# A planned instruction order in which GpSimd and VectorE take turns

## The chip, the core and the metric

The kernel runs on one core of a Trainium2 chip. The metric is the device time of one execution, in microseconds. Before the change it was 10084.26 us, the median of three runs (10083.36 to 10087.48). The engines are called by their names or as the profile abbreviates them: PE is TensorE (matrix products and transposes), PEld its weight loads, DVE is VectorE, ACT is ScalarE, POOL is GpSimd, SP is SyncE, which issues the transfers.

## What is computed

The input is a batch of 8 images of 256 channels and 32 x 32 points, in float32. Four layers follow each other, each on the output of the one before:

- Layer 0: a normalisation over channels, attention with 4 heads over the 1024 points (with a 3 x 3 depthwise convolution of the values added as positional term) and a projection, added to the input; then a second normalisation, a 1 x 1 convolution to 1024 channels, a 3 x 3 depthwise convolution, a gelu gate, a 1 x 1 convolution back to 256 channels, and a filter in the Fourier domain of 8 x 8 patches, added again.
- Layer 1: group normalisation, attention with 8 heads, projection, and a small two-layer network with gelu, each with a residual.
- Layer 2: a bottleneck of 1 x 1, 3 x 3 and 1 x 1 convolutions on values rounded to 8 bits, with a residual.
- Layer 3: a selective state-space scan in four directions over the points of each image (rows and columns, forward and backward), with 512 inner channels and 16 states each. For each state the recurrence h[t] = h[t-1] * exp(dt[t] * A) + dt[t] * u[t] * B[t] runs over the points, and the output is the sum over states of h[t] * C[t]. The four directions are summed.

## The kernel before

The work is cut into two phases that follow each other. `phase_a` takes the 8 images ("samples") through layers 0, 1 and 2 and leaves the 8-bit codes of each in DRAM. `phase_b` does layer 3.

The order of the instructions is not the order of the source. Each piece of work is a Python generator (a strand) that yields operations; class `_Order` holds all strands and makes the lists of all engines while the program is built. Each operation is an `_Op` (line 103): an engine, what it reads and writes, and `cost`, its expected duration in microseconds. The price is a formula in n, the largest number of columns of an operand divided by 1024, chosen by engine and kind of operation (lines 112 to 136). `start` (line 237) gives the earliest planned time of an operation: the engine must be free, and what it reads and overwrites must be done, with a latency for what another engine did. `run` (line 306) always emits the operation with the smallest planned start, and among equals the one of the smaller rank, then advances the engine's free time by the price. `keep_dense` (line 269) adds filler matmuls (line 295, weights `minus`) where the plan leaves TensorE idle for long. On the chip each engine then works through its list in order, and waits on semaphores only for data and buffers; the planned times are not in the program.

In phase A up to three samples are under way at once. The eight PSUM banks (`bank`) are shared by the attention and by everything else. For the softmax, `maxima` (line 603) computes scores into banks, VectorE takes their maxima from there (`stats`), ScalarE the exponentials in place; `exponentials` (line 669) computes the scores again with the maximum subtracted, takes exponentials into `exps`, and sums values into a bank. Where such a sum is complete, `finish` (line 799) in layer 0 adds it to the positional term: on VectorE if that term is ready, otherwise by way of a ScalarE copy and a GpSimd addition into `big`. The 3 x 3 depthwise convolutions are sums of nine shifted and scaled images. `outer_taps` (line 738) does a tap on two engines, a ScalarE scaling into `mid` and a GpSimd addition; it serves the positional term (tile `big`) and two of the eight chunks of the feed-forward part (tile `mid`). The other six chunks (line 888) do a tap in one VectorE `scalar_tensor_tensor` on tiles `mid`, of 31 x 31 = 961 or 992 columns. The normalisations (`rms`, line 519) and the rounding of layer 2 are VectorE work on SBUF too.

In phase B there are 64 blocks (8 images, 4 directions, 2 halves of 512 points), each of 16 groups, one per state. For a group, ScalarE makes `dbu` and `da`, TensorE transposes `dbu` into PSUM (`db`), VectorE scans four times 512 points (`h`), GpSimd multiplies h by C in two instructions of 1024 columns (line 1585), and TensorE sums the products into `py`. Between these run the preparations of the next blocks, through the PSUM tile `pp`: projections, a causal convolution with a VectorE `scalar_tensor_tensor` that reads PSUM, dt and its softplus, and the copies to `du`.

Of the kernel before, what the change touches and what calls it, by code (L numbers as in the profile page):

```python
# [22 lines left out]
BF16 = mybir.dt.bfloat16  # L23
# [3 lines left out]
PSUM = bass.MemoryType.PSUM  # L27
# [46 lines left out]
@with_exitstack  # L74
def tile_conv_seq(ctx: ExitStack, tc: tile.TileContext, i: dict, out: bass.AP):
    nc = tc.nc
    const = ctx.enter_context(tc.tile_pool(name="const", bufs=1))


    cols = const.tile([P, NCOL], F32, name="cols", tag="cols")  # L80
    nc.sync.dma_start(cols, i["cols"])

    def col(name, k=0, n=1):
        a = _AT[name][0] + k
        return cols[:, a : a + n]

    ident = const.tile([P, P], F32, name="ident", tag="ident")
    make_identity(nc, ident)
    dram = ctx.enter_context(tc.tile_pool(name="cd", bufs=1, space=DRAM))
    codes = [  # L90
        [dram.tile([CC, P, N], BF16, name=f"codes{b}_{k}", tag=f"codes{b}_{k}") for k in range(2)] for b in range(B)
    ]

    parts = [dram.tile([P, CC, 3, P], BF16, name=f"w_in{m}", tag=f"w_in{m}") for m in range(2 * DC)]

    phase_a(tc, i, col, ident, codes, parts)
    phase_b(tc, i, col, ident, codes, parts, out)


class _Op:  # L100


    def __init__(self, engine, method, args, kw):
        self.engine, self.method, self.args, self.kw = engine, method, args, kw
        out, ins = args[0], [a for a in (*args[1:], *kw.values()) if isinstance(a, bass.AP)]
        self.reads = {k for a in ins for k in self.blocks(a)}
        self.writes = {k for a in (out, kw.get("accum_out")) if a is not None for k in self.blocks(a)}
        self.landing = 0.0
        n = max(math.prod(a.shape[1:]) for a in (out, *ins)) / 1024
        near = all(a.space == out.space and out.space != PSUM for a in ins)  # L110
        points = sum(math.prod(a.shape[1:]) == 1 for a in ins)
        if engine == "tensor":
            x = kw.get("rhs", ins[0])
            n = math.prod(x.shape[1:]) / 1024
            self.rows = x.shape[0] / P * n * (0.427 if x.dtype != F32 else 1.707)
            move = method == "transpose" or kw.get("is_transpose", False)
            self.cost = max(0.05, n * (0.427 if x.dtype != F32 else 0.854 if move else 1.707))
            self.rows *= 0.5 if move else 1
        elif engine == "vector":
            fast = near and method in ("tensor_scalar", "tensor_copy")  # L120
            both = near and method == "tensor_tensor"
            three = near and method == "scalar_tensor_tensor"
            if method == "tensor_tensor_scan":
                self.cost = 0.03 + 2.15 * n + 0.05 * points
            elif both or three:
                self.cost = 0.04 + 1.53 * n
            elif fast:
                self.cost = 0.04 + 0.87 * n
            else:
                self.cost = 0.05 + 1.12 * n + 0.06 * min(points, 1)  # L130
        elif engine == "scalar":
            self.cost = 0.04 + 0.054 * near + 0.852 * n + 0.093 * points + 0.1 * ("accum_out" in kw)
        elif engine == "gpsimd":
            self.cost = 0.12 + 2.3 * n if method == "tensor_tensor" else 0.07 + (2.0 if out.dtype == BF16 else 1.5) * n
        else:
            self.cost, self.landing = 0.06, 3.6

# [12 lines left out]
class _Table:  # L150


    engine, reads, writes, cost, landing = "scalar", set(), set(), 1.3, 0.0

    def emit(self, nc):
        nc.scalar.preload_act_table_set("natural_log_exp_and_others")  # L156
# [27 lines left out]
class _Order:  # L184
# [7 lines left out]
    def __init__(self, nc):  # L192
        self.nc, self.strands, self.n = nc, [], 0
        self.free, self.written, self.read, self.base, self.last = {}, {}, {}, {}, {}
        self.rooms, self.minus, self.way, self.rows, self.fresh = [], None, 0.0, [], {}
        self.window, self.dense, self.half = 0, 0.0, False

    def add(self, rank, strand):
        self.n += 1
# [36 lines left out]

    def start(self, ops):
        e = ops[0].engine
        t = self.free.get(e, 0.0)
        for o in ops:  # L240
            for k in o.reads | o.writes:
                t = max(t, self.base.get(k[0], 0.0))
                w, by = self.written.get(k[0], {}).get(k, (0.0, e))
                t = max(t, w + (self.LATENCY[by] if by != e else 0.0))
            for k in o.writes:
                w, by = self.read.get(k[0], {}).get(k, (0.0, e))
                t = max(t, w + (self.LATENCY[by] if by != e else 0.0))
        return t
# [57 lines left out]
    def run(self):  # L306
        while self.strands:
            moved = True
            while moved:
                moved = False  # L310
                for s in list(self.strands):
                    if callable(s[2]) and s[2]():
                        self.go(s)
                        moved = True
            ready = [s for s in self.strands if not callable(s[2])]
            if not ready:
                assert not self.strands, [s[0] for s in self.strands]
                return
            t, s = min(((self.start(s[2][1]), s) for s in ready), key=lambda x: (x[0], x[1][0]))
            cost, ops = s[2]  # L320
            e = ops[0].engine
            if self.rooms and e == "tensor":
                t, cost = self.keep_dense(t, cost, ops)
            for o in ops:
                o.emit(self.nc)
                for k in o.reads:
                    self.read.setdefault(k[0], {})[k] = (t + cost + 0.7 * o.landing, e)
                for k in o.writes:
                    self.fresh.pop(k[0], None)
                    self.written.setdefault(k[0], {})[k] = (t + cost + o.landing, e)  # L330
            self.free[e] = t + cost
            self.go(s)


@with_exitstack
def phase_a(ctx, tc, i, col, ident, codes, w_parts):
# [783 lines left out]
    class _Table:  # L1120


        engine, reads, writes, cost, landing = "scalar", set(), set(), 1.3, 0.0

        def emit(self, nc):
            nc.scalar.preload_act_table_set("natural_log_exp_and_others")
# [675 lines left out]
```

## Time and profile before

| what | before |
| --- | --- |
| median of three runs | 10084.26 us |
| the profiled execution's own time | 10081.69 us |
| its span, first to last instruction | 10079.9 us |
| mean granted TensorE clock | 0.974 |
| busy: PE, ACT, DVE, POOL | 92%, 84%, 78%, 61% |
| phase A, to about 3540 us: PE, ACT, DVE, POOL busy | 3290, 2614, 2287, 954 us |
| phase B, 6540 us: PE, ACT, DVE, POOL busy | 6033, 5898, 5538, 5227 us |

An engine's busy time is the time in which at least one of its instructions runs; matmuls overlap each other, and the fillers count as busy. A line of a group of instructions names the source line (147 for all that the planner emits), the engine, the operation, the tiles as out<-in, their shapes, and the count; then the busy time in us and the mean duration of one in ns; then the engine's idle time just before these instructions, and what ended it. A window's line gives its bounds, its length, the busy time of each engine with the number of instructions, the granted TensorE clock, the share of the transfer engines, and GB/s. The slices are fortieths of the span; a digit is the busy share in tenths.

### The profile page before, as it was taken

Reading aid. Unit: us, or ns where it says so; the run is one execution under the profiler, and the core shown is the slowest. Engines: PE = TensorE matmul, PEld = TensorE weight load, DVE = VectorE, ACT = ScalarE, POOL = GpSimd, SP = SyncE. Lnnn points to the kernel's source line nnn. Section 1 sums busy time; section 2 is a strip of 40 time slices with the busy share of each in tenths; the row PEclk is TensorE's granted clock in tenths of the full one; section 3 lists DMA queues with packets and bytes.
Section 4 is the critical chain, followed back from the end, with each engine's and each line's share of the span. In section 5 each row is a group of like instructions: output and inputs, shape, how many; then the busy total and the mean of one; then the engine's idle time right before and its main releaser. Section 6 shows DMA issues by size and latency. Waiting matters only on the chain.

```text
span 10079.9 us, 152800 instructions
## 1 busy us (share of the span) xinstructions
PE 9322.4 (92%) x56655; PEld 5929.6 (59%) x56777; DVE 7825.8 (78%) x8666; ACT 8512.0 (84%) x15878; POOL 6180.5 (61%) x2998
## 2 busy tenths in 40 slices
PE   9988989989999989999999999999999999999998
PEld 3333333333333357777777777777777777777776
DVE  6476586586666568888888888888888888888788
ACT  8987765868677679998999998999898999898998
POOL 1454023142211068887878787878787878787888
PEclk9999999999999999999999999999999999999999
DMA  2100000000000011111111111112111111111111
GB/s 60 36 27 25 7 22 14 18 27 17 13 18 18 9 49 50 52 50 55 53 45 61 46 53 54 49 50 60 44 56 49 55 50 50 55 52 47 58 44 54
DMA packets 219628, 416.01 MB, mean 41 GB/s; under 512 B 25137, under 2 KB 67505, under 8 KB 213762
## 3 DMA queue, kind: packets, MB, share of 16 engines
q1 hardware_dynamic: 218882, 406.24, 13.1%
q8 instruction: 447, 7.32, 0.3%
q14 instruction: 299, 2.45, 0.1%
HBM read 358.43 MB, written 37.22 MB: 39 GB/s over the span
## 4 chain that ended last, share of the span: by engine, by line
PE 28%; ACT 22%; DVE 11%; issue 3%; DMA 1%; POOL 1%; DVEq 0%; SPq 0%; POOLq 0%; ACTq 0%
PE pp L147 12%; DVE h L147 9%; ACT da L147 9%; PE py L147 8%; PE db L147 8%; ACT dbu L147 7%; ACT L147 2%; ACT xs L147 2%; ACT dt L147 1%; DMA wi<-w_in 1%; ACT L156 1%; DVE du L147 1%; POOL h L147 1%; ACT st L147 0%; DVE ys L147 0%
## 5 line engine op out<-in xcount | busy, mean ns | idle before, releaser
L147 POOL TENSOR_TENSOR h<-h,cb 128x1024 f32<-128x1024 f32 x2048 | 4813.4, 2374 | 971.5 <-DVE h L147 441.0
L147 ACT ACTIVATE da<-dt,am 128x512 f32<-128x512 f32 x4096 | 2873.3, 714 | 452.2 <-DVE h L147 444.3
L147 ACT ACTIVATE dbu<-du,bT 128x512 f32<-128x512 f32 x4096 | 2800.5, 709 | 53.2 <-PE db L147 48.3
L147 PE MATMUL db<-ident,dbu 128*128 128x128 f32 x16384 | 2400.5, 278 | 390.2 <-DVE h L147 336.1
L147 DVE TENSOR_TENSOR_SCAN h<-da,db 128x512 f32<-128x512 f32 x2048 | 2344.5, 1201 | 439.4 <-ACT da L147 181.6
L147 DVE TENSOR_TENSOR_SCAN h<-da,st,db 128x512 f32<-128x512 f32 x2048 | 2465.1, 1260 | 263.2 <-ACT da L147 153.6
L147 PEld LDWEIGHTS db<-ident,dbu 128*128 128x128 f32 x16384 | 1871.7, 142 | 950.7 <-DVE h L147 526.5
L147 PE MATMUL py<-ident,h 128*128 128x128 f32 x16384 | 2095.8, 274 | 34.1 <-POOL h L147 33.2
L147 PEld LDWEIGHTS py<-ident,h 128*128 128x128 f32 x16384 | 1849.6, 141 | 97.0 <-POOL h L147 55.4
L147 DVE TENSOR_REDUCE stats<-bank 128x1 f32<-128x512 f32 x1536 | 972.0, 681 | 400.7 <-PE bank L147 394.2
L147 ACT ACTIVATE bank<-bank,stats 128x512 f32<-128x512 f32 x1536 | 1025.4, 714 | 266.6 <-DVE stats L147 261.7
L147 POOL TENSOR_TENSOR mid<-mid,mid 128x961 f32<-128x961 f32 (+2 forms) x192 | 402.3, 2103 | 966.9 <-ACT mid L147 661.9
L147 ACT ACTIVATE exps<-bank 128x512 f32<-128x512 f32 x1536 | 801.9, 636 | 144.8 <-PE bank L147 143.8
L147 PE MATMUL bank<-big,big 32*128 32x512 f32 x4096 | 845.0, 650 | 14.4 <-ACT bank L147 8.4
L147 PE MATMUL pp<-xi,cvd 128*128 128x512 f32 x1488 | 687.9, 598 | 6.3 <-DVE dt L147 6.3
L147 DVE SCALAR_TENSOR_TENSOR mid<-mid,cols,mid 128x961 f32<-128x961 f32 (+1 forms) x384 | 629.2, 1639 | 5.9
L147 PE MATMUL bank<-exps,big 128*32 128x512 f32 (+1 forms) x3072 | 565.2, 627 | 0.7 <-ACT exps L147 0.6
L147 PEld LDWEIGHTS bank<-big,big 32*128 32x128 f32 x4096 | 295.6, 187 | 429.8 <-issue 213.2
L147 POOL TENSOR_SCALAR big<-big,ga,gs 128x512 f32<-128x512 f32 x64 | 74.5, 1176 | 750.6 <-DVE gs L147 292.5
L147 POOL TENSOR_TENSOR tmp<-dt,xs 128x512 f32<-128x512 f32 x256 | 322.8, 1272 | 320.5 <-ACT dt L147 209.6
L147 POOL TENSOR_TENSOR big<-big,mid 128x961 f32<-128x961 f32 (+1 forms) x128 | 326.2, 2556 | 302.1 <-ACT mid L147 279.9
L295 PEld LDWEIGHTS <-minus 128*128 128x128 bf16 x2233 | 210.0, 101 | 446.7 <-issue 263.2
(207 smaller groups left out, 9792.7 us busy)
## 6 DMA issues: line engine op xcount, KB each, us to landing
cb<-c_d SPq DMA_DIRECT2D x1024, 256.0 KB, 3.2
wi<-w_in SPq DMA_DIRECT2D x192, 192.0 KB, 3.5
big<-in_x_dram SPq DMA_DIRECT2D x16, 1024.0 KB, 5.3
kept<-big SPq DMA_DIRECT2D x16, 1024.0 KB, 4.3
big<-kept SPq DMA_DIRECT2D x16, 1024.0 KB, 4.8
xf<-codes SPq DMA_DIRECT2D x48, 256.0 KB, 4.1
big<-big SPq DMA_DIRECT2D x16, 512.0 KB, 6.4
codes<-low SPq DMA_DIRECT2D x32, 256.0 KB, 2.0
```

The costliest lines, as they stand in the source:

```text
L147: return getattr(getattr(nc, self.engine), self.method)(*self.args, **self.kw)
L156: nc.scalar.preload_act_table_set("natural_log_exp_and_others")
L295: self.nc.tensor.matmul(x, lhsT=self.minus, rhs=rhs, start=True, stop=True)
```

## The change

The planner gets other prices, and one more resource. Each operation has a new attribute `port`. It is true for all GpSimd operations, and for those VectorE operations whose operands of more than one column all lie in SBUF (for a scan, the output is not looked at; the statistics of the group normalisation are left out). `start` lets an operation with `port` begin no earlier than the end of the last one with `port`, of whichever of the two engines, and `run` keeps that end. Prices change for VectorE operations on SBUF alone (two tensor inputs; scalar operations and copies), and for GpSimd's two-tensor operations. The kernel's computations, tiles, buffers and transfers are not edited.

```diff
@@ -105,7 +105,7 @@
         out, ins = args[0], [a for a in (*args[1:], *kw.values()) if isinstance(a, bass.AP)]
         self.reads = {k for a in ins for k in self.blocks(a)}
         self.writes = {k for a in (out, kw.get("accum_out")) if a is not None for k in self.blocks(a)}
-        self.landing = 0.0
+        self.landing, self.port = 0.0, engine == "gpsimd"
         n = max(math.prod(a.shape[1:]) for a in (out, *ins)) / 1024
         near = all(a.space == out.space and out.space != PSUM for a in ins)
         points = sum(math.prod(a.shape[1:]) == 1 for a in ins)
@@ -117,21 +117,23 @@
             self.cost = max(0.05, n * (0.427 if x.dtype != F32 else 0.854 if move else 1.707))
             self.rows *= 0.5 if move else 1
         elif engine == "vector":
+            wide = [a for a in ins if math.prod(a.shape[1:]) > 1] + [out] * (method != "tensor_tensor_scan")
+            self.port = not method.startswith("bn_") and all(a.space != PSUM for a in wide)
             fast = near and method in ("tensor_scalar", "tensor_copy")
             both = near and method == "tensor_tensor"
             three = near and method == "scalar_tensor_tensor"
             if method == "tensor_tensor_scan":
                 self.cost = 0.03 + 2.15 * n + 0.05 * points
             elif both or three:
-                self.cost = 0.04 + 1.53 * n
+                self.cost = 0.06 + 1.11 * n
             elif fast:
-                self.cost = 0.04 + 0.87 * n
+                self.cost = 0.05 + 0.56 * n + 0.05 * min(points, 1)
             else:
                 self.cost = 0.05 + 1.12 * n + 0.06 * min(points, 1)
         elif engine == "scalar":
             self.cost = 0.04 + 0.054 * near + 0.852 * n + 0.093 * points + 0.1 * ("accum_out" in kw)
         elif engine == "gpsimd":
-            self.cost = 0.12 + 2.3 * n if method == "tensor_tensor" else 0.07 + (2.0 if out.dtype == BF16 else 1.5) * n
+            self.cost = 0.12 + 2.2 * n if method == "tensor_tensor" else 0.07 + (2.0 if out.dtype == BF16 else 1.5) * n
         else:
             self.cost, self.landing = 0.06, 3.6
 
@@ -150,7 +152,7 @@
 class _Table:
 
 
-    engine, reads, writes, cost, landing = "scalar", set(), set(), 1.3, 0.0
+    engine, reads, writes, cost, landing, port = "scalar", set(), set(), 1.3, 0.0, False
 
     def emit(self, nc):
         nc.scalar.preload_act_table_set("natural_log_exp_and_others")
@@ -193,7 +195,7 @@
         self.nc, self.strands, self.n = nc, [], 0
         self.free, self.written, self.read, self.base, self.last = {}, {}, {}, {}, {}
         self.rooms, self.minus, self.way, self.rows, self.fresh = [], None, 0.0, [], {}
-        self.window, self.dense, self.half = 0, 0.0, False
+        self.window, self.dense, self.half, self.port = 0, 0.0, False, 0.0
 
     def add(self, rank, strand):
         self.n += 1
@@ -236,7 +238,7 @@
 
     def start(self, ops):
         e = ops[0].engine
-        t = self.free.get(e, 0.0)
+        t = max(self.free.get(e, 0.0), self.port if ops[0].port else 0.0)
         for o in ops:
             for k in o.reads | o.writes:
                 t = max(t, self.base.get(k[0], 0.0))
@@ -329,6 +331,8 @@
                     self.fresh.pop(k[0], None)
                     self.written.setdefault(k[0], {})[k] = (t + cost + o.landing, e)
             self.free[e] = t + cost
+            if ops[0].port:
+                self.port = t + cost
             self.go(s)
 
 
@@ -1120,7 +1124,7 @@
     class _Table:
 
 
-        engine, reads, writes, cost, landing = "scalar", set(), set(), 1.3, 0.0
+        engine, reads, writes, cost, landing, port = "scalar", set(), set(), 1.3, 0.0, False
 
         def emit(self, nc):
             nc.scalar.preload_act_table_set("natural_log_exp_and_others")
```

What the built program's lists become, in counts: phase A has 1163 filler matmuls where there were 1299, phase B 992 where there were 934. Six of the 64 attention sums of layer 0 that VectorE added are copied by ScalarE and added by GpSimd instead. All other instructions are the same in number. Position by position and without the fillers, another instruction stands in 4487 of TensorE's 6754 places in phase A, and in 10235 of its 39296 in phase B; for VectorE in 2240 of 3290 and 789 of 5378, for ScalarE in 2560 of 4193 and 2666 of 10151, for GpSimd in 339 of 485 and 10 of 2518.

## The prediction

> **What bounds the kernel now.** I read the page's slices first: where they change character, phase A (samples through layers 0 to 2) gives way to phase B (the scans of layer 3).
>
> ```profile
> PE   9988989989999989999999999999999999999998
> DVE  6476586586666568888888888888888888888788
> ACT  8987765868677679998999998999898999898998
> POOL 1454023142211068887878787878787878787888
> ...
> PE 28%; ACT 22%; DVE 11%; issue 3%; DMA 1%; POOL 1%; DVEq 0%; SPq 0%; POOLq 0%; ACTq 0%
> ```
>
> POOL jumps in slice 15, at about 3540 us. The chain of waits (last line) starts there too, so it speaks for phase B alone: 66% of the span, PE, ACT and DVE taking turns, POOL 1%. Phase A is read from its windows: all instructions, then L295 alone (filler matmuls that the list puts where it expects TensorE idle). Columns: window, length, PE, PEld, DVE, ACT, POOL busy.
>
> ```profile
> 500.00:1000.00 500.00, 441.67 (x1871) 170.65 (x1865) 351.62 (x355) 385.09 (x735) 250.33 (x112) 0.92 0.08 27
> 1000.00:1250.00 250.00, 243.47 (x1264) 93.56 (x1259) 142.88 (x260) 198.46 (x502) 8.05 (x8) 0.97 0.03 9
> 2000.00:2250.00 250.00, 222.38 (x826) 84.90 (x828) 201.71 (x234) 161.80 (x321) 115.47 (x52) 0.91 0.08 27
> 0.00:3540.00 3540.00, 3289.76 (x15267) 1235.20 (x15267) 2287.37 (x3289) 2614.47 (x5728) 953.94 (x480) 0.95 0.07 22
> ...
> 0.00:3540.00 3540.00, 356.33 (x1299) 116.58 (x1299) 0.95 0.07 22
> 3540.00:10080.00 6540.00, 231.88 (x934) 93.43 (x934) 0.99 0.17 52
> ```
>
> TensorE is the fullest engine of phase A: 3290 of 3540 us, but 356 of these are filler, so it does useful work for 2933 us, 82.9%. The fillers of the shorter windows were 37.53, 32.77 and 25.58 us, so the useful share is (441.67-37.53)/500 = 80.8% in 500:1000, where POOL is half busy; 84.3% in 1000:1250, where POOL is idle; and 78.7% in 2000:2250. That is the loss the change bears on. Its cause is in VectorE's groups, over all of phase A, then in 1000:1250 (POOL idle), then in 556:577 (POOL working almost throughout):
>
> ```profile
> L147 DVE SCALAR_TENSOR_TENSOR mid<-mid,cols,mid 128x961 f32<-128x961 f32 x192 | 317.4, 1653 | 3.0
> L147 DVE SCALAR_TENSOR_TENSOR mid<-mid,cols,mid 128x992 f32<-128x992 f32 x192 | 311.8, 1624 | 2.9
> L147 DVE TENSOR_SCALAR mid<-mid,cols 128x1024 f32<-128x1024 f32 x64 | 70.8, 1106 | 148.2 <-ACT mid L147 106.2 <-POOL mid L147 35.6 <-ACT low L147 5.2
> ...
> L147 DVE SCALAR_TENSOR_TENSOR mid<-mid,cols,mid 128x992 f32<-128x992 f32 x8 | 9.9, 1241 | 0.0
> L147 DVE SCALAR_TENSOR_TENSOR mid<-mid,cols,mid 128x961 f32<-128x961 f32 x8 | 9.7, 1208 | 0.0
> L147 DVE TENSOR_SCALAR mid<-mid,cols 128x1024 f32<-128x1024 f32 x2 | 1.5, 748 | 2.4 <-ACT mid L147 2.4
> ...
> L147 DVE SCALAR_TENSOR_TENSOR mid<-mid,cols,mid 128x992 f32<-128x992 f32 x4 | 10.7, 2669 | 0.1
> ```
>
> The same tap takes 1241 ns alone and 2669 beside POOL. Excess over the undisturbed rows: 192x(1653-1208) = 85, 192x(1624-1241) = 74, 64x(1106-748) = 23; the 64 normalising products (mean 1129 ns, against 750 for the same operation on 512 columns from PSUM) add 24. Together 206 us in which VectorE stands still, and behind it the maxima that free PSUM banks: ScalarE waits 261.7 us for `stats`, TensorE's weight loads 230.8 us for ScalarE to be done with `bank`.
>
> **The change, part by part.** (1) *The turns.* The list now keeps one port time for GpSimd and for those VectorE instructions whose wide operands all lie in SBUF. Nothing enforces this on the chip: no wait is added, only the order changes. All of phase B's planned VectorE instructions read PSUM, so there the rule binds nothing. The Trainium skill, "SBUF — State Buffer", section "Who interferes with whom", calls the shared port an exclusive lock: the loser blocks for the other's whole instruction, and an instruction with one SBUF input, outside the two-port modes, does not contend. Rows first: 1241 against 2669 agrees with blocking, and the scans, which read one operand from PSUM, hold 1201 and 1260 ns while POOL is 80% busy. By the rule this speaks against the change: a lock moves waiting from one engine to the other and makes no port time. So I do not book the 206 us; by "collisions vanish" the sum would be -206, by the rule it is only what TensorE gets out of better neighbours. Three readings of that. (a) Bringing 500:1000 and 2000:2250 to the 84.3% of the POOL-free window: 404.1/0.843 = 479 and 196.8/0.843 = 233, that is -21 and -17, -37 us. (b) All of phase A at 84.3%: 2933/0.843 = 3480, -60. (c) The new instruction list has 1163 fillers in phase A for 1299, all other TensorE work the same in count: 136 x 274 ns (356.3/1299) = -37; were the unfilled idle time (3540-3290 = 250) to fall in proportion, 26 more, -63. I take **-45**, nearer to the -37 that two readings share. Ends: -63, and +40 (useful share down by one point, less than half the spread between windows: 2933/0.819 = 3581), since two thirds of phase A's TensorE positions hold another instruction than before (4487 of 6754, fillers aside), with the same buffers.
>
> (2) *New prices of VectorE.* An SBUF tap goes from 0.04+1.53n to 0.06+1.11n thousandths of a column count n/1024: 1.48 to 1.10 us at 961 columns; a scalar operation on 1024 from 0.91 to 0.66. The undisturbed rows, 1208 and 748, lie some 0.1 above the new prices, as does the untouched maximum (681 ns, priced 0.61). So these now tell undisturbed time evenly. Their effect is the same reordering as (1), and is in its sum.
>
> (3) *One branch decided otherwise.* An attention sum is added by VectorE if the positions are complete, else by a ScalarE copy and GpSimd. 6 of 64 sums change side: VectorE 6x0.69 = -4 us, ScalarE 6x0.60 = +4, GpSimd 6x1.47 = +9. GpSimd idles over 70% of phase A and ScalarE a quarter, which hides it: 0; uncovered, +13.
>
> (4) *GpSimd's price, 2.42 to 2.32 us for a product of 1024.* It is what moves phase B: GpSimd's order there hardly changes (10 positions of 2518), but 26% of TensorE's and ScalarE's positions do. In the timeline ten products run in 23.45 us, 2.345 each: the old price was 0.075 high, the new one is 0.025 low. The sums over h (`py`) therefore stand earlier in TensorE's in-order queue, and when they are early, the transposes behind them (`db`, which feed the scans) wait too. TensorE's waits for POOL's h are 33.2 us, its weight loads' 55.4. Worst: each of 2048 products exposes 0.025, +51; I take +4. Fillers in phase B rise from 934 to 992: 58 x 248 ns (231.9/934) = +14 if all lie on the path; at TensorE's share of the chain, 28 of 66, +6. Best end: -25, should truer prices remove a quarter of the 88 us of waits. I take **+10**, ends -25 and +65.
>
> No DMA, table load or semaphore wait of another kind is added; the transfers are the same in count and size. Sum: -45 + 0 + 10 = -35 us on the profiled execution's own 10081.7 (span 10079.9, 1.8 around it), 10047; the median shown is 2.6 above that execution, so 10049, said as **10050**.
>
> **Rivals.** *Slower: GpSimd's chain in phase A is held up.* Each sample's positional taps are 16 adds on GpSimd; held behind a 1.24 us tap in the list, they may start up to 1.24 later each: 20 us a sample, 159 over eight, and projection waits for them. For it: the 6 sums of part 3, which found the positions incomplete. Against: POOL idles long before `big` adds (222.3 us for ScalarE alone), and TensorE waits for POOL's big only 48.9 us. It cancels part 1 from 45/8 = 5.6 us a sample, five held adds. Half of it on the path: 10049+80 = 10129. *No change: the list's turns are lost on the chip.* With no lock in the program, an error of 1 us, one instruction's length, undoes a turn, and the taps stay near 1640 ns. For it: phase A's engines wait for each other up to 60 us at a time. Then only noise and part 4 remain: 10084 to 10094. *Larger gain: reading (c) in full and phase B's best end:* 10084-63-25 = 9996; it belongs to the first case's range.
>
> **How the numbers follow.** Forecast 0.48 (own range 9996 to 10063), no change 0.21, slower rival 0.31. 0.2% is 20 us, about what a measurement of this kernel can tell from no change. So faster 0.48, same 0.21, slower 0.31. The bounds of the parts give 9996 to 10084+40+65 = 10189; leaving one in ten on either side, 9990 to 10130.
>
> **What would show it.** Right: taps' means in phase A at 1350 to 1500 ns, about 1163 fillers, GpSimd's first scan product some 45 us earlier, a useful share near 84%, phase B 6540 to 6560 us. Wrong: taps still above 1600 (turns not kept); taps short but phase A no shorter (the time was not TensorE's); TensorE's or ScalarE's wait for POOL's big well over 48.9 us (the slower rival); or phase B off by over 40 us, 0.6 us for each of its 64 blocks, which part 4 could not price.

## The result and the profile after

The changed kernel takes 9933.94 us (median of four runs, 9917.28 to 9939.44), against 10085.87 us for the kernel before, measured beside it. The ratio is 0.9846, with a 95% interval of 0.9829 to 0.9863: 1.5% faster. The direction was forecast, the size was not: 152 us where 35 were expected, and below the stated range of 9990 to 10130.

The profiled execution has a span of 9933.8 us, 146.1 less than before. The first view is the page of the changed kernel: the slices, and the chain by engine.

```profile
PE   9999999999999899999999999999999999999998
DVE  6458657567776388888888888888888888888888
POOL 1452123232220178887887878887887888787888
...
PE 28%; ACT 26%; DVE 8%; issue 2%; POOL 1%; DMA 1%; another core or an unknown queue 0%; SPq 0%; DVEq 0%; POOLq 0%; ACTq 0%
```

TensorE's slices of phase A, which were 8 or 9, are now all 9 but one. To cut the span in two, take the end of GpSimd's last copy of codes (`low<-low`) in the timeline (start, duration, instruction; before, then after):

```profile
3537.19 1.88 POOL L147 COPY low<-low 128x1024 bf16<-128x1024 bf16 x1 [2.37 <-issue]
3416.02 1.88 POOL L149 COPY low<-low 128x1024 bf16<-128x1024 bf16 x1 [2.37 <-issue]
```

Phase A ended at 3539.1 us before and ends at 3417.9 after. It lost 121.2 us; what follows it went from 6540.8 to 6515.9, 24.9 less. The windows of the changed kernel by phase come next: all instructions, then the fillers alone (columns: window, length, PE, PEld, DVE, ACT, POOL busy, clock, transfer share, GB/s).

```profile
0.00:3418.00 3418.00, 3214.22 (x15131) 1217.27 (x15131) 2192.24 (x3283) 2619.27 (x5734) 907.26 (x486) 0.96 0.07 23
3418.00:9934.00 6516.00, 6039.20 (x41439) 4703.64 (x41568) 5533.09 (x5377) 5900.21 (x10150) 5225.99 (x2518) 0.99 0.17 52
...
0.00:3418.00 3418.00, 326.27 (x1163) 105.33 (x1163) 0.96 0.07 23
3418.00:9934.00 6516.00, 244.12 (x992) 99.09 (x992) 0.99 0.17 52
```

In phase A TensorE's useful time is 3214.2-326.3 = 2888 us, 84.5% of 3418. Its share rose by 1.6 points from 82.9%, and the useful time itself fell by 45 us from 2933, though the matmuls, fillers aside, are the same. Phase A's 121 us are then 45 of useful time, 30 of fillers (356 to 326) and 46 in which TensorE was idle (250 to 204). VectorE is busy 95 us less, and GpSimd 47 less (954 to 907): the waiting did not move from one of the two to the other, it went down on both. VectorE's groups, in phase A of the changed kernel:

```profile
L149 DVE SCALAR_TENSOR_TENSOR mid<-mid,cols,mid 128x992 f32<-128x992 f32 x192 | 273.2, 1423 | 3.3
L149 DVE SCALAR_TENSOR_TENSOR mid<-mid,cols,mid 128x961 f32<-128x961 f32 x192 | 270.0, 1406 | 3.5
L149 DVE TENSOR_SCALAR mid<-mid,cols 128x1024 f32<-128x1024 f32 x64 | 66.7, 1042 | 68.5 <-ACT mid L149 46.2 <-POOL big L149 9.8 <-issue 9.3
```

The taps fell from 1653 and 1624 ns to 1406 and 1423, of which 1208 and 1241 are needed. A little over half of the excess is gone.

### The profile page after: what moved, and what is told of

It is laid out like the page before. It is cut to its first block, busy times and chain, and to the rows that moved or that the text cites. A ratio compares the mean times of both kernels' runs of the same rounds, so it can differ in the third digit from the quotient of the medians.

```text
span 9933.8 us, 152509 instructions
## 1 busy us (share of the span) xinstructions
PE 9253.4 (93%) x56570; PEld 5920.9 (60%) x56699; DVE 7725.3 (78%) x8660; ACT 8519.5 (86%) x15884; POOL 6133.2 (62%) x3004
## 4 chain that ended last, share of the span: by engine, by line
PE 28%; ACT 26%; DVE 8%; issue 2%; POOL 1%; DMA 1%; another core or an unknown queue 0%; SPq 0%; DVEq 0%; POOLq 0%; ACTq 0%
PE pp L149 12%; ACT da L149 11%; ACT dbu L149 9%; PE py L149 8%; PE db L149 8%; DVE h L149 7%; ACT L149 2%; ACT xs L149 2%; ACT dt L149 1%; ACT L158 1%; POOL h L149 1%; DMA wi<-w_in 1%; ACT st L149 1%; DVE du L149 0%; DVE ys L149 0%
## 5 line engine op out<-in xcount | busy, mean ns | idle before, releaser
L149 PE MATMUL db<-ident,dbu 128*128 128x128 f32 x16384 | 2368.0, 278 | 346.2 <-DVE h L149 310.2
L149 DVE TENSOR_TENSOR_SCAN h<-da,st,db 128x512 f32<-128x512 f32 x2048 | 2465.4, 1263 | 275.0 <-ACT da L149 153.6
L149 ACT ACTIVATE bank<-bank,stats 128x512 f32<-128x512 f32 x1536 | 1024.8, 693 | 247.8 <-DVE stats L149 241.8
L149 DVE SCALAR_TENSOR_TENSOR mid<-mid,cols,mid 128x961 f32<-128x961 f32 (+1 forms) x384 | 543.2, 1415 | 6.8
L149 PE MATMUL bank<-exps,big 128*32 128x512 f32 (+1 forms) x3072 | 545.0, 615 | 0.8 <-ACT exps L149 0.7
L149 POOL TENSOR_TENSOR tmp<-dt,xs 128x512 f32<-128x512 f32 x256 | 322.8, 1272 | 324.4 <-ACT dt L149 206.2
```

The costliest lines, as they stand in the source:

```text
L149: return getattr(getattr(nc, self.engine), self.method)(*self.args, **self.kw)
```

## The experiments

The theory after the result: blocked VectorE instructions hold up far more of phase A than was booked, and the port rule avoids them (theory 1 in the expectations, "the turns"). Its rivals: the list needed truer prices, with or without turns (theory 2); or any new list of phase A may land anywhere, and this one was lucky (theory 3). In phase B the question was what made it faster at all. The table collects all runs. "A ends" is the end of GpSimd's last copy of codes, "rest" the span after it, "taps" the mean of all 384 VectorE taps, which for 961 and 992 columns needs about 1225 ns. "Median" is one run where no ratio is given. All times are us, the taps ns. The columns from "A ends" on come from one traced execution each, and executions scatter: those of the kernel before lie between 10076 and 10095, and the same list of phase A, traced again, ended at 3539, 3542 and 3547 (before and the last two rows) and at 3395 and 3398 (the turns with old prices). The traced executions of `gpsimd_price_only` and `sums_early` were 10 and 8 us slower than their medians, that of `prices_no_turns` 11 us faster. A difference under some 20 us between two traces is not read as an effect.

| run | median | ratio to before (95%) | A ends | rest | taps | fillers in A |
| --- | --- | --- | --- | --- | --- | --- |
| before | 10084 | | 3539.1 | 6540.8 | 1639 | 1299 |
| after | 9933.9 | 0.9846 (0.9829 to 0.9863) | 3417.9 | 6515.9 | 1415 | 1163 |
| turns_old_prices | 9948.7 | 0.9866 (0.9851 to 0.9880) | 3397.6 | 6548.7 | 1388 | 1525 |
| prices_no_turns | 10097.6 | 1.0012 (1.0006 to 1.0019) | 3565.0 | 6520.2 | 1568 | 1188 |
| gpsimd_price_only | 10024.7 | 0.9942 (0.9927 to 0.9956) | 3506.2 | 6526.3 | 1557 | 1272 |
| before_tap_150 | 10096.7 | | 3552.7 | 6542.2 | 1633 | 1340 |
| tap_130_turns | 9952.5 | | 3405.8 | 6544.9 | 1402 | 1501 |
| tap_116 | 9981.0 | | 3463.1 | 6516.0 | 1430 | 1347 |
| turns_b_price | 9913.8 | 0.9831 (0.9814 to 0.9847) | 3394.7 | 6517.8 | 1383 | 1525 |
| before_writes | 9924.7 | | 3378.6 | 6544.3 | 1316 | 1299 |
| before_writes_long | 10037.3 | | 3488.6 | 6546.9 | 1295 | 1299 |
| after_writes | 9857.8 | | 3341.0 | 6515.0 | 1263 | 1163 |
| sums_early | 10095.3 | 1.0011 (1.0005 to 1.0018) | 3546.7 | 6554.9 | 1640 | 1299 |
| price_sums_late | 10071.5 | 0.9985 (0.9978 to 0.9992) | 3542.4 | 6527.8 | 1640 | 1299 |

### One part of the change alone

`turns_old_prices`, against the changed kernel:

```diff
-                self.cost = 0.06 + 1.11 * n
+                self.cost = 0.04 + 1.53 * n
-                self.cost = 0.05 + 0.56 * n + 0.05 * min(points, 1)
+                self.cost = 0.04 + 0.87 * n
-            self.cost = 0.12 + 2.2 * n if method == "tensor_tensor" else ...
+            self.cost = 0.12 + 2.3 * n if method == "tensor_tensor" else ...
```

> The port rule of the change alone, with the old prices (phase B's list is that of before). Theory 1, the turns: collisions between VectorE's taps and GpSimd's additions cost phase A its time, and only the port rule avoids them: most of the 122 us comes, 9960 to 10000 us in all, taps near 1400 ns. Theory 2, the prices: the list mostly needs the undisturbed durations; with turns priced at disturbed durations the taps are counted twice, so it is no faster than before, 10070 to 10150, although the taps are short. Theory 3, a re-deal: any new list may land anywhere, 9950 to 10150, and the tap's mean tells nothing of it.

`prices_no_turns`, against the changed kernel:

```diff
-        t = max(self.free.get(e, 0.0), self.port if ops[0].port else 0.0)
+        t = self.free.get(e, 0.0)
```

> The change's prices alone, without the port rule (phase B's list is that of the changed kernel). Theory 1: taps stay near 1640 ns, phase A stays at 3520 to 3550 us, in all 10050 to 10070 with phase B's 22 us. Theory 2: phase A near 3420 to 3450, in all 9935 to 9970, with taps still long. Theory 3: anywhere from 9930 to 10130.

`gpsimd_price_only`, against the kernel before:

```diff
-            self.cost = 0.12 + 2.3 * n if method == "tensor_tensor" else ...
+            self.cost = 0.12 + 2.2 * n if method == "tensor_tensor" else ...
```

> Only GpSimd's two-tensor price, 2.3 to 2.2 per 1024. Phase B's list is then that of the changed kernel: it should take 22 us less than before from the first scan to the end, if the price is the cause there. In phase A theories 1 and 2 expect no gain (3530 to 3550 us, in all 10055 to 10075); theory 3 expects any phase A between 3400 and 3600, since its list is dealt anew as well.

VectorE's taps, first with the turns alone, then with the prices alone:

```profile
L149 DVE SCALAR_TENSOR_TENSOR mid<-mid,cols,mid 128x961 f32<-128x961 f32 x192 | 266.7, 1389 | 2.8
L149 DVE SCALAR_TENSOR_TENSOR mid<-mid,cols,mid 128x992 f32<-128x992 f32 x192 | 266.2, 1387 | 2.9
```

```profile
L149 DVE SCALAR_TENSOR_TENSOR mid<-mid,cols,mid 128x992 f32<-128x992 f32 x192 | 309.3, 1611 | 3.5
L149 DVE SCALAR_TENSOR_TENSOR mid<-mid,cols,mid 128x961 f32<-128x961 f32 x192 | 292.9, 1525 | 3.8
```

The turns alone end phase A at 3397.6 us, 141.5 earlier, and 20 earlier than the whole change. The prices alone end it at 3565.0, 26 later than before, with taps still long. With the new prices the turns are worth 147.1 (3565.0 to 3417.9), with the old ones 141.5. Phase A's gain therefore belongs to the turns, and theory 2 falls: the turns worked although the taps were priced at the blocked duration. In these three runs no forecast of theory 1 was met in size: the turns alone came out 11 us below their band, and the prices alone 28 us above theirs in the whole. In the third run phase A ended 33 us earlier where theories 1 and 2 expected nothing. Its price is also that of phase A's additions, and its taps are 5% shorter, so fewer collisions may be part of it; that was not separated. Theory 3 may have a part too: lists may differ by some tens of us for no reason of their own. The next three runs measure how many.

### Neighbouring lists

`before_tap_150` sets 0.04 + 1.50n for 1.53n in the kernel before; `tap_130_turns` sets 1.30 for 1.53 in the run with turns and old prices; `tap_116` sets 0.06 + 1.16n for 1.11n in the changed kernel.

```diff
-                self.cost = 0.04 + 1.53 * n
+                self.cost = 0.04 + 1.50 * n
```

> The kernel before with VectorE's two-input price at 0.04+1.50n for 1.53n, and no turns. A neighbour that re-deals phase A's list without a reason to be better. Theory 1: taps near 1600 ns, phase A 3500 to 3570. Theory 3: anything from 3380 to 3570.

> The port rule with the old prices, but VectorE's two-input operations at 0.04+1.30n, between old and new. Shows how far phase A scatters over lists that all take turns (3398 and 3418 so far). Theory 1: 3380 to 3440 us, in all 9930 to 9990 with the old list of phase B. Theory 3: anything from 3380 to 3570.

> The changed kernel with VectorE's two-input price at 0.06+1.16n for 1.11n, nearer to the undisturbed row, turns kept. Theory 1: phase A 3380 to 3440 and taps near 1400 ns, 9910 to 9960 in all. Theory 3: anything from 3380 to 3570.

Four different lists without turns end phase A at 3506, 3539, 3553 and 3565 us (mean 3541); four with turns at 3398, 3406, 3418 and 3463 (mean 3421). The groups do not overlap. The means lie 120 us apart, with a 95% interval of about 72 to 167 from the scatter of the eight, and within a group lists spread over 60 to 65 us. `before_tap_150` and `tap_130_turns` fell in theory 1's bands; `tap_116` overshot its band of 3380 to 3440 by 23, although its price is nearer to the undisturbed row than that of the change. Among the four with turns, phase A ends later the longer the taps are (1388, 1402, 1415 and 1430 ns); among the four without, it does not. So the 121 us of the change lie within what turns are worth, and the 20 us between the whole change and its turns alone are within what any two lists differ by.

### Collisions taken away without touching the list

In `before_writes` and `after_writes` the list is the old or the new one, instruction for instruction, but each GpSimd tap is emitted as two memsets of the tile that it would have read, and an addition of one column. GpSimd is as busy as before, but it writes instead of reading. The sums of these taps are left out.

```diff
-            yield G.tensor_tensor(o, o, img(t)[to], ALU.add)
+            op = G.tensor_tensor(o, o, img(t)[to], ALU.add)
+            def emit(nc, o=o, t=t, s=img(t)[to]):
+                nc.gpsimd.memset(t, 0.0)
+                nc.gpsimd.memset(t, 0.0)
+                nc.gpsimd.tensor_tensor(o[:, :, :1], o[:, :, :1], s[:, :, :1], ALU.add)
+            op.emit = emit
+            yield op
```

> The list of before, unchanged, but each GpSimd tap addition is emitted as two memsets of the 128x1024 tile that it would read, and an addition of one column (the taps' sums are left out). By the row of the 1024-column memset (951 ns) the GpSimd time stays about 2.1 us a tap, but GpSimd writes and hardly reads. If reading is what blocks VectorE's taps of two SBUF inputs, they fall to about 1250 ns and phase A shows what collisions cost in the list of before: theory 1 expects 60 to 120 us less (3420 to 3480), theories 2 and 3 under 30 us. If the taps stay near 1640 ns, writes block as well and the run tells nothing of the theories.

> The list of the changed kernel with each GpSimd tap addition emitted as two memsets and an addition of one column (the taps' sums are left out). If the collisions are what separates the two lists, phase A falls from 3418 to about 3360 to 3390 us, close to the 3379 of the old list with writes: 30 to 60 us gained where the old list gained 160. If the new list is better for another reason (theory 3), it keeps its lead of 120 us: about 3260.

A stretch of the timeline of `before_writes`, GpSimd first, then VectorE (start, duration, instruction):

```profile
1666.92 0.95 POOL L748 MEMSET mid<- 128x1024 f32 x1
1667.93 1.38 POOL L749 MEMSET mid<- 128x1024 f32 x1
1669.40 0.91 POOL L750 TENSOR_TENSOR big<-big,mid 128x31 f32<-128x31 f32 x1
1670.24 0.95 POOL L748 MEMSET mid<- 128x1024 f32 x1
1671.25 0.95 POOL L749 MEMSET mid<- 128x1024 f32 x1
```

```profile
1667.02 1.41 DVE L147 TENSOR_SCALAR mid<-mid,cols 128x1024 f32<-128x1024 f32 x1 [6.31 <-POOL mid L147]
1668.35 0.67 DVE L147 TENSOR_REDUCE stats<-bank 128x1 f32<-128x512 f32 x1
1668.94 1.20 DVE L147 SCALAR_TENSOR_TENSOR mid<-mid,cols,mid 128x961 f32<-128x961 f32 x1
1670.07 0.68 DVE L147 TENSOR_REDUCE stats<-bank 128x1 f32<-128x512 f32 x1
1670.67 2.49 DVE L147 SCALAR_TENSOR_TENSOR mid<-mid,cols,mid 128x992 f32<-128x992 f32 x2
```

Two taps in a row run beside two memsets at 1.24 us each, and neither side is slowed. The scalar operation, with one input, takes 1.41 us beside a memset (748 ns alone), and the memset behind it 1.38. The one-column addition, which reads, takes 0.91 us while the tap at 1668.94 runs.

The windows of phase A, old list and then new list with writes:

```profile
0.00:3380.00 3380.00, 3215.24 (x15267) 1216.75 (x15267) 2075.54 (x3289) 2608.34 (x5728) 911.48 (x992) 0.97 0.07 23
0.00:3341.00 3341.00, 3177.11 (x15131) 1203.50 (x15131) 2048.79 (x3283) 2614.57 (x5734) 884.36 (x998) 0.97 0.07 24
```

With the old list, unchanged, phase A ends at 3378.6 us, 160.5 earlier (theory 1 expected 60 to 120): that is what reading instead of writing cost it, but for a small part that the next run sizes. VectorE's busy time in phase A falls from 2287.4 to 2075.5, by 212, so a blocked microsecond of VectorE costs this list about 0.75. ScalarE's waits for `stats` fall from 261.7 to 176.1 us, and those of TensorE's weight loads for ScalarE's `bank` from 230.8 to 194.0; the maxima behind the blocked taps are thus on the path. The changed list, which has less than half the excess, gains 76.9 by the same replacement and ends at 3341.0 (expected: 3360 to 3390), 0.54 us for each of 143 us of VectorE (2192.2 to 2048.8); the price of a blocked microsecond is no constant. Without collisions the new list leads by 38 us instead of 121. So some 84 of the 121 us are shown to be collisions, the difference of the two gains; the other 38 are within the spread of lists, and the new list is not shown to be better in any other way.

`before_writes_long` puts in a third memset, to see whether GpSimd's slightly shorter taps (busy 911.5 us for 953.9) did it:

```diff
+                nc.gpsimd.memset(t, 0.0)
```

> The list of before with three memsets and an addition of one column for each GpSimd tap addition (the taps' sums are left out), so that GpSimd works about 3.3 us a tap, a third longer than with the real additions. If the blocked reads were what phase A lost, it stays at 3380 to 3420 us though GpSimd is slower than ever; if GpSimd's own chain was the limit (the 160 us of the run with two memsets coming from its slightly shorter taps), it goes to 3540 or above.

The third memset adds 249.1 us of GpSimd time, and phase A ends at 3488.6. Neither alternative was right. The collisions are gone (taps 1295 ns) and 50 us are gained against the list of before although GpSimd works longer, but 110 are lost again: GpSimd's own chain is on the path too, at 110/249 = 0.44 us a microsecond. Applied to the 42 us that the two memsets saved, this explains about 19 of the 160 us, which leaves 0.67 us for a blocked microsecond of VectorE.

### Phase B

All six runs with the old list of phase B have a rest of 6540.8 to 6548.7 us; all six with the new one, 6515.0 to 6526.3. The means lie 26 us apart, whatever phase A did, and `gpsimd_price_only` against before, like `turns_b_price` against the turns with old prices, changes nothing but GpSimd's price there: GpSimd's price is the cause. The two runs that follow ask what it does. `sums_early` leaves the price old and sets the latency that the list counts behind GpSimd from 0.1 to 0.0, which moves the sums forward and may move whatever else waits for GpSimd; `price_sums_late` has the new price and a latency of 0.2. Both change phase B alone.

```diff
+    _Order.LATENCY = {**_Order.LATENCY, "gpsimd": 0.0}
```

> The kernel before, with the list's latency behind GpSimd 0.0 instead of 0.1 us in phase B alone; GpSimd's price stays old. TensorE's sums over h then stand about as early as under the new price. If their earlier place, which frees the h tiles sooner, is what gained 24 us in phase B, then phase B takes 15 to 30 us less than 6471 and the whole 10055 to 10070; if GpSimd's pace in the list is what counts, 10080 to 10090.

> The kernel before, with GpSimd's new price in phase B alone, and the list's latency behind GpSimd 0.2 instead of 0.1 us there, which puts the sums back to where the old price had them. Early sums as the cause: no gain, phase B 6460 to 6480 and 10080 to 10090 in all. GpSimd's pace in the list as the cause: 10055 to 10070.

With the sums early and the old price phase B gains nothing (6554.9 in a trace 8 us over its median; the whole 0.11% slower, above both forecasts). With the new price and late sums it keeps half of the gain (6527.8; 13 of the 26 us; the whole 0.15% faster). So an earlier place of the sums is not the cause by itself; GpSimd's truer pace in the list is part of it. Waits in 3650:9850, a stretch of equal length in both though phase B begins 121 us earlier in the changed kernel, before and then after:

```profile
DVE h L147 <- PE py L147: 184.0, 174, 4.3
...
PEld py L147 <- POOL h L147: 41.7, 76, 1.0
...
PE py L147 <- POOL h L147: 23.3, 39, 0.8
```

```profile
DVE h L149 <- PE py L149: 128.2, 137, 3.9
...
PEld py L149 <- POOL h L149: 72.8, 138, 1.8
...
PE py L149 <- POOL h L149: 40.0, 77, 1.3
```

TensorE waits more for GpSimd, as forecast, 113 us for 65. But the scans wait less for TensorE to give `h` tiles back, 128 us for 184. Which of the moved positions brings the 26 us stays open: in `sums_early` that wait of the scans fell as well, to 157.5, and nothing was gained.

### A version that is faster than both

`turns_b_price` joins the better phases: turns with VectorE's old prices, and GpSimd's new price in phase B alone.

```diff
 class _Op:
+    pool = 2.3
-            self.cost = 0.12 + 2.3 * n if method == "tensor_tensor" else ...
+            self.cost = 0.12 + self.pool * n if method == "tensor_tensor" else ...
 # first line of phase_b
+    _Op.pool = 2.2
```

> The port rule with VectorE's old prices, GpSimd's old price in phase A and its new price in phase B. Phase A's list is that of the run with turns and old prices, phase B's that of the changed kernel. If the two phases add up, 9948.7-24 = 9925 us (9918 to 9932); the changed kernel took 9933.9.

9913.8 us, ratio 0.9831 (0.9814 to 0.9847), 11 below the expected sum. It leads the changed kernel by 20 us in the medians; the intervals of the two ratios overlap, and in phase A 20 us are within the spread of lists.

## Why the prediction was wrong

The direction and the cause were right: collisions on the shared port, thinned out by the list, in phase A; taps of 1350 to 1500 ns (1415 measured). The slower rival and the rival without effect are out. The waits of TensorE's weight loads for POOL's `big`, which were to show the slower rival, fell (in 0:3400, before and then after):

```profile
PEld bank L147 <- POOL big L147: 45.4, 36, 3.8
PEld bank L149 <- POOL big L149: 12.5, 18, 2.4
```

Its premise, that GpSimd's chain lies on the path, holds all the same: 0.44 us a microsecond in `before_writes_long`.

- Part 1, the turns, is the step that failed: -45 booked, with an end at -63. The port rule alone measured -141.5, the whole change -121.2. The rule of the lock was read as a reason not to book the 206 us of VectorE's excess. The step "a lock moves waiting from one engine to the other" is what did not hold: the order decides whether the two meet at all, and VectorE and GpSimd both became less busy, by 95 and 47 us. The replacement by writes measured 0.54 us (new list) to 0.75 us (old list) of phase A for a blocked microsecond of VectorE; the forecast amounted to 45/206 = 0.22. The waits that the prediction named did not show the gain in the change itself: ScalarE's for `stats` fell only from 261.7 to 241.8 us, and the weight loads' for `bank` rose from 230.8 to 247.3. By which waits the 121 us came is not shown.
- Readings (a) and (b) held TensorE's useful time fixed and let only its share rise. The share of (b), 84.3%, was nearly met (84.5%). But 2933 us became 2888, which makes 2888/0.845 = 3418 instead of 3480. The same matmuls ran faster, with the granted clock at 0.96 for 0.95 (0.948 and 0.963 from the clock records of the traces: 1.5%, as much as the useful time fell). Two groups of phase A up to 3400, before and then after:

```profile
L147 PE MATMUL bank<-exps,big 128*64 128x512 f32 x1024 | 267.4, 644 | 0.6 <-ACT exps L147 0.6
...
L147 PE MATMUL bank<-big,w_pi 128*128 128x512 f32 x512 | 263.7, 643 | 10.1 <-ACT bank L147 9.6 <-DVE low L147 0.5
```

```profile
L149 PE MATMUL bank<-exps,big 128*64 128x512 f32 x1024 | 253.2, 617 | 0.7 <-ACT exps L149 0.7
...
L149 PE MATMUL bank<-big,w_pi 128*128 128x512 f32 x512 | 252.7, 620 | 7.4 <-ACT bank L149 7.3
```

  The records show a clock that is either full or half. Of the first group, matmuls wholly at full clock took 605 ns before and 604 after, those wholly at half clock 1077 and 1072; what changed is that 80 of 1024 ran wholly at half clock before and 20 after. The Trainium skill, "TensorE: Matmul & The Clock Gate", Part 1, says that the clock is gated by how busy the array has lately been. The traces agree: TensorE idle for 250, 204 and 158 us of phase A (before, after, the turns alone) goes with a clock of 0.948, 0.963 and 0.974. In the turns alone (0:3398, fillers 407.8 us) the useful time is 2833 us, 3.4% below that of before, at a clock 2.8% higher:

```profile
0.00:3398.00 3398.00, 3240.46 (x15493) 1225.56 (x15493) 2128.36 (x3283) 2619.75 (x5734) 895.97 (x486) 0.97 0.07 23
```

  That such a gain adds to the idle time saved was not in the sum: in the change it is 45 of the 121 us.
- Reading (c), in full -63 and only in its first term the -37 that it was said to share with (a), took fewer fillers for less time. Its two terms came out in the change, 30 us of fillers for 37 and 46 us of idle time for 26, but the count forecasts nothing: the turns alone have 1525 of them, more than before, and a shorter phase A than the change with 1163.
- Part 2, the prices, went into part 1's sum. Alone they moved phase A by +26 us, within the spread of lists, and no gain of them in phase A is shown.
- Part 3 was 0, and no run tests it. At the rate of `before_writes_long` its 9 us on GpSimd would cost about 4.
- Part 4, phase B, had the wrong sign: +10 booked, -24.9 measured. That this is the stated best end of -25 is luck: that end supposed a quarter of TensorE's waits for GpSimd removed, and they grew. That they grew is what the +4 expected, but phase B became shorter all the same. The filler term (+6) failed with it: 58 more fillers, 12 us more of them (231.9 to 244.1), and a shorter phase B.

## What to carry to other kernels

When two engines share a port, price a blocked microsecond by what is queued behind the blocked engine, here among others the maxima that free PSUM banks. A comparison of TensorE's useful share between windows put the loss at 45 us, where the turns alone gave back 141 and the replacement by writes 160. To size such a loss before an edit, keep the order and replace the reading instruction by a writing one of the same length. And where a planner deals thousands of instructions, judge a change of it against neighbours, lists made by small edits of prices: here they lay up to 65 us apart, half of the effect.

## What the runs showed of the hardware

- A VectorE instruction with two SBUF inputs is blocked by a GpSimd instruction that reads SBUF and not by one that writes it: 1.24 us beside memsets, 2669 ns on average in a stretch full of GpSimd additions. A scalar operation with one input, 748 ns alone, took 1.41 us beside a memset. The Trainium skill, "SBUF — State Buffer", section "Who interferes with whom", says so for two inputs, and the runs agree. It also says that two-port modes contend in general; that this scalar operation runs in such a mode no run here shows.
- TensorE's clock was granted in full or by half, and a matmul of 128x512 in float32 took 604 or about 1075 ns accordingly (the group `bank<-exps,big`, as the profile records it). With TensorE idle for 204 us of phase A instead of 250, fewer matmuls ran at half clock (20 of 1024 for 80 in one group), and the means of two groups fell by about 4%. A sum over idle time misses this gain.
